# A transformer block: contexts turned and two head pairs' context keys projected before the self-attention, the last key block's values made in two pieces

## The chip, the cores and the metric

The kernel runs on one core of one Trainium2 chip. The time is that of one execution on the device, in microseconds. TensorE (PE, with its weight loads PEld) multiplies and turns, VectorE (DVE), ScalarE (ACT) and GpSimd (POOL) do the rest, and the DMA queues of SyncE (SP) and ScalarE load and store.

## The reference

Everything is float32. x is (2, 1024, 256): two sequences of 1024 tokens. The context is (2, 154, 192). With 16 heads of 64:

```
h = layernorm(x, ln1);  x = attention(h, h,       sa_wq, sa_wk, sa_wv, sa_wo, sa_bo) + x
h = layernorm(x, ln2);  x = attention(h, context, ca_wq, ca_wk, ca_wv, ca_wo, ca_bo) + x
h = layernorm(x, ln3);  a, gate = split(h @ ff_w1 + ff_b1)
out = (a * gelu(gate)) @ ff_w2 + ff_b2 + x
```

Attention is softmax(q k^T / 8) v per head. The keys and values of the second attention are projections of the context alone (ca_wk, ca_wv: 192 x 1024), so they depend on nothing that the first attention computes.

## The kernel before

The heads go in pairs, eight pairs for each of two sequences: 16 units. A unit of self-attention has eight slots, each of which makes the scores of two groups of queries against all 1024 keys (`scores`, L526, two buffers), takes the maximum on VectorE (L712), the exponents on ScalarE (L537), exchanges maxima and sums between partitions by four small DMAs on SyncE (L547), scales on GpSimd (L650) and turns on VectorE (L675). Beside this TensorE does, in an order written out by hand, the work that other slots left: projections of the next unit's queries, keys and values (L369, L405, L431), the product with the values (L578), the output projection (L500). `run_work` takes, in a slot, from a list `work` first and then one entry of a list `side`. An engine executes its instructions in the order in which the program issues them.

Before the first slot stands a beginning of its own. x comes in four loads of two tiles each on the queues of SyncE and ScalarE (`load_x`), then the gain and shift of the first normalisation, element by element into the columns `cols` (L110), then the weights. DMAs take turns over eight semaphores, so that each one is issued only when the eighth before it has landed. TensorE passes the time with 27 transposes of the identity (L1293). `norm_pieces` gives the statistics (L242, L243), the deviation (L248, L252), the normalising (L273 on GpSimd, L276 on ScalarE) and the turning (L286) with the copy to hT (L297 on VectorE, L301 on ScalarE) for pairs of tiles, and the beginning issues these in between the first unit's queries and keys, for a quarter of the tokens at a time (`part`, in the banks `first` and `first_k`).

The context enters as follows. `turn_context` turns both sequences' contexts into ctxT (L203), `context_keys` projects one pair's keys into kT (L792), and `turn_rows` (L194) turns the rows of the other gains and biases into columns. These stand in `side` for the first four slots. Of a context's 154 rows the last block of 32 is kept apart: `context_ends` (L813) projects it for both sequences and both halves of the heads, 128 columns at a time, into `ends`; its weights come by `load_ends` (L803), both in the self-attention's units 5 to 8 (L1355 to L1360), a piece in the seventh slot of each.

`xt[1, 1]` (the second half of the second sequence's x) is loaded only from the second unit on, and `held_v[:, 1]` and `held_v[:, 3]` (values) are first written in the first two units.

Of the kernel before, what the change touches and what calls it, by code (L numbers as in the profile page):

```python
# [13 lines left out]
P = 128  # L14
# [4 lines left out]
def tile_transformer_block(ctx: ExitStack, tc: tile.TileContext, a: dict, out: bass.AP):  # L19
# [19 lines left out]
    KP = T // 2  # L39
    KB = 32  # L40
    NB = -(-T // KB)
    EC = P
    VC = 2 * P
    HB = 512
    QG = 2 * KB
# [34 lines left out]
        for b in range(B) for g in range(NG)  # L80
    }

    def load_x(queue, b, t):

        queue.dma_start(
            out=xt[b, t // GT][:, t % GT:t % GT + 2, :],
            in_=x[b, t * P:(t + 2) * P, :].rearrange("(t p) d -> p t d", p=P),
        )

# [12 lines left out]
            n_cols = r + k  # L102
        r += k
    rows = pp_.tile([n_rows - n_cols, P], F32, tag="P", name="rows")
    for t in range(0, NT // 2, 2):
        load_x(nc.sync, 0, t)
        load_x(nc.scalar, 0, NT // 2 + t)
    for n in names[:2]:
        for r0 in range(0, P, HR):
            (nc.scalar if n == names[0] else nc.sync).dma_start(  # L110
                out=cols[r0:r0 + HR, row_of[n]:row_of[n] + NH],
                in_=w[n].rearrange("(r p) -> p r", p=HR),
            )
    bias = {}

    def load_bias(n):
# [56 lines left out]
    cn = []  # L173
    for b in range(B):
        cn.append(pp_.tile([KP, 2, DC], F32, tag="P", name=f"cn{b}"))
        nc.sync.dma_start(out=cn[b], in_=cond[b].rearrange("(t p) d -> p t d", p=KP))
    load_bias("sa_bo")

    power = const.tile([P, 2], F32, tag="power", name="power")
    nc.gpsimd.memset(power, -0.5)  # L180
    ident = const.tile([P, P], F32, tag="ident", name="ident")
    make_identity(nc, ident)

# [27 lines left out]


    ends = const.tile([P, DA // 2], F32, tag="ends", name="ends")
    held_v = const.tile([P, 4, NT, P], F32, tag="held_v", name="held_v")

    hT, vs, qk, oT = {}, {}, {}, {}

# [577 lines left out]
            )  # L795
        return lambda: nc.scalar.copy(kT[:, pr, :], pk[:, :B * TP])

    def load_ends(f, n):

        t = wpool.tile([CC, 2, 2, n], F32, tag="ck", name=f"ca_wv_{f}")  # L800
        own = w["ca_wv"].rearrange("(c p) (h f) -> p c h f", p=CC, h=2)
        for c in range(2):
            nc.sync.dma_start(out=t[:, c], in_=own[:, c, :, f:f + n])  # L803
        wsl["ends", f] = t

    def context_ends(f, n, bank):

        pe = bank(f"pe_{f}")
        for c in range(2):
            for b in range(B):  # L810
                for half in range(2):
                    r0 = (2 * b + half) * KB
                    nc.tensor.matmul(  # L813
                        pe[r0:r0 + KB, :n], lhsT=ctxT[:, c, (b + 1) * TP - KB:(b + 1) * TP],
                        rhs=wsl["ends", f][:, c, half, :], start=(c == 0), stop=(c == 1),
                        tile_position=(0, r0),
                    )
        return lambda: nc.scalar.copy(ends[:, f:f + n], pe[:, :n])
# [447 lines left out]
    with tc.manual_schedule():  # L1266
# [3 lines left out]
        def emit(*pieces):  # L1270
            for piece in pieces:
                run(piece)
            flush(stores)
# [15 lines left out]
                      i * P, 2 * P, shared=True)  # L1289


        for _ in range(27):
            nc.tensor.transpose(own[0][:, 1, :P], ident, ident)  # L1293
# [30 lines left out]
        work.extend(unit_value_piece(*units[0], i, 2) for i in (0, 2))  # L1324

        for p in range(SA):
# [26 lines left out]
            else:  # L1353
                run_work(2 if p < SA - SH else 1, h % 2 or h == 0, sum_tile)
            if hg == LAG:  # L1355
                f = (ui - NPAIR // 2 - 1) * EC
                if n == LAG and 0 <= f < DA // 2:
                    load_ends(f, min(EC, DA // 2 - f))
                elif n == SH + LAG and 0 <= f < DA // 2:
                    run(lambda: context_ends(f, min(EC, DA // 2 - f), sum_tile))  # L1360
                if n == SH + LAG and ui in (0, 1, NU - 1):

                    pr = {0: 2, 1: 4, NU - 1: 6}[ui]
                    run(lambda: context_keys(pr, sum_tile))
                    kept.append(context_keys(pr + 1, mm_tile))
# [175 lines left out]
```

## Time and profile before

| | us |
|---|---|
| median of 3 runs | 1068.17 (1067.32 to 1068.81) |
| profiled execution | 1067.09 |
| its span | 1065.1 |
| TensorE busy | 1055.6 (99%) |
| VectorE busy | 882.5 (83%) |
| GpSimd busy | 778.4 (73%) |
| ScalarE busy | 647.3 (61%) |
| DMA | 57 GB/s in the mean |

Times in the profile count from the span's start; the profiled execution is the span and what lies around it. The chain of waits follows the work that ended last back from the last instruction, at each step to what released it; a change shows in the end only where it touches this chain. In the timeline a row is a group of like instructions in a row: its start, its length, engine, line, operation, tiles, count, and in brackets how long the engine had been idle and what released it. The ends of matmuls are modelled, so a busy TensorE can hide a short wait. The granted clock of TensorE reads 1.00 in every stretch.

### The profile page before, as it was taken

To read this page: it belongs to the slowest core of one execution; us is meant where nothing else is said; L and a number is where in the kernel's file an instruction comes from. 1 tells how busy PE (TensorE), PEld (TensorE's weight loads), DVE (VectorE), ACT (ScalarE), POOL (GpSimd) and SP (SyncE) were. 2 spreads that over 40 slices of the span, in tenths; PEclk is the share of its full clock that TensorE was granted. 3 is DMA by queue.
4 is the path that set the end of the run, shared out by engine and by line. 5 is a ranking of instruction groups with operands and counts; after the bars stand their busy time and mean duration, and the time that the engine had idled before them with its cause. 6 is when DMAs were issued, how large, how long until landed. Compare 5 with 4: busy or idle time off the path is not lost.

```text
span 1065.1 us, 48669 instructions
## 1 busy us (share of the span) xinstructions
PE 1055.6 (99%) x20228; PEld 707.7 (66%) x20228; DVE 882.5 (83%) x1321; ACT 647.3 (61%) x2096; POOL 778.4 (73%) x1652
## 2 busy tenths in 40 slices
PE   8999999999999999999999999999999999999998
PEld 6556656656555555667655655566866668788998
DVE  5789999998989989999999899979877877654555
ACT  5766767677666666666776676666666554343231
POOL 2677777778777777777777777777767875499984
PEclk9999999999999999999999999999999999999999
DMA  3131122121021121111102101126776545000000
GB/s 102 36 75 54 29 68 54 25 63 41 22 58 28 34 51 34 39 34 34 45 14 54 44 14 38 33 57 161 175 172 165 123 98 125 5 11 11 21 10 30
DMA packets 86046, 60.95 MB, mean 57 GB/s; under 512 B 32123, under 2 KB 74563, under 8 KB 85827
## 3 DMA queue, kind: packets, MB, share of 16 engines
q1 hardware_dynamic: 84450, 57.07, 22.1%
q8 instruction: 159, 2.61, 1.0%
q10 hardware_dynamic: 1376, 0.79, 0.3%
q14 instruction: 61, 0.49, 0.2%
HBM read 27.91 MB, written 2.10 MB: 28 GB/s over the span
## 4 chain that ended last, share of the span: by engine, by line
PE 90%; DVE 3%; POOL 2%; DMA 2%; SPq 1%; issue 1%; ACT 1%; DVEq 0%; POOLq 0%; ACTq 0%
PE po L578 19%; PE s L526 19%; PE py_ca L500 5%; PE py_sa L500 5%; PE pk_sa L369 5%; PE pq_sa L369 5%; PE pq_ca L369 4%; PE pv_sa L405 4%; PE poc L953 4%; PE pb L1074 4%; PE pq L1219 4%; PE sc L873 3%; PE pa L1074 2%; PE pc L1074 2%; PE pf L1249 1%; PE ph_ln L286 1%
## 5 line engine op out<-in xcount | busy, mean ns | idle before, releaser
L650 POOL TENSOR_SCALAR p<-p,rd,ee 128x512 f32<-128x512 f32 x512 | 392.6, 772 | 88.6 <-DVE rd L640 86.6
L537 ACT ACTIVATE p<-s,st 128x512 f32<-128x512 f32 x512 | 345.3, 687 | 174.1 <-DVE st L712 170.6
L712 DVE TENSOR_REDUCE st<-s 128x2 f32<-128x1024 f32 x256 | 308.7, 1207 | 57.7 <-issue 17.5
L675 DVE STREAM_TRANSPOSE pT<-p 128x1024 f32<-128x1024 f32 x256 | 302.5, 1219 | 1.6 <-POOL p L650 1.4
L526 PE MATMUL s<-k_sa,q_sa 64*32 64x512 f32 x4096 | 255.8, 591 | 0.8 <-DVE k_sa L390 0.6
L578 PE MATMUL po<-pT,held_v 64*32 64x256 f32 x8192 | 238.9, 376 | 0.0
L578 PEld LDWEIGHTS po<-pT,held_v 64*32 64x32 f32 x8192 | 178.2, 106 | 69.8 <-issue 26.5
L526 PEld LDWEIGHTS s<-k_sa,q_sa 64*32 64x32 f32 x4096 | 87.4, 106 | 93.1 <-issue 46.8
L890 ACT ACTIVATE p<-sc,neg 128x154 f32<-128x154 f32 x256 | 96.4, 406 | 73.5 <-DVE rden L898 70.6
L901 POOL TENSOR_SCALAR p<-p,rden 128x154 f32<-128x154 f32 x256 | 97.3, 401 | 47.3 <-DVE rden L898 47.0
L537 ACT ACTIVATION_READ_ACCUMULATOR p<-s,st 128x1 f32 x512 | 103.7, 203 | 0.0
L555 POOL TENSOR_TENSOR dd<-st 128x8 f32<-128x8 f32 x128 | 25.8, 202 | 69.0 <-DMA st<-st 65.1
L500 PE MATMUL py_ca<-ca_wo,o_ca 128*128 128x256 f32 x256 | 60.2, 383 | 0.0
L500 PE MATMUL py_sa<-sa_wo,o_sa 128*128 128x256 f32 x256 | 59.5, 386 | 0.0
L500 PEld LDWEIGHTS py_sa<-sa_wo,o_sa 128*128 128x128 f32 x256 | 47.3, 190 | 18.0 <-issue 5.9
L369 PE MATMUL pq_ca<-hT_ln,ca_wq 64*64 64x512 f32 (+1 forms) x576 | 58.5, 589 | 0.3 <-DMA ca_wq<-in_L_xattn_ca_wq_dram 0.3
L879 DVE TENSOR_REDUCE neg<-sc 128x6 f32<-128x924 f32 (+1 forms) x48 | 47.8, 995 | 12.1 <-PE sc L873 12.1
L369 PE MATMUL pq_sa<-hT_ln,sa_wq 64*32 64x512 f32 (+1 forms) x976 | 57.3, 586 | 0.0
L890 ACT ACTIVATION_READ_ACCUMULATOR p<-sc,neg 128x1 f32 x256 | 56.7, 221 | 0.0
L369 PE MATMUL pk_sa<-hT_ln,sa_wk 64*32 64x512 f32 x960 | 56.5, 590 | 0.1
L917 DVE STREAM_TRANSPOSE pT_ca<-p 128x480 f32<-128x480 f32 (+1 forms) x96 | 52.9, 586 | 0.9 <-POOL p L901 0.8
L500 PEld LDWEIGHTS py_ca<-ca_wo,o_ca 128*128 128x128 f32 x256 | 47.4, 190 | 8.2 <-issue 1.9
(158 smaller groups left out, 1479.5 us busy)
## 6 DMA issues: line engine op xcount, KB each, us to landing
wf<-pT_ca SPq DMA_DIRECT2D x128, 128.0 KB, 2.4
st<-st SPq DMA_DIRECT2D x512, 1.0 KB, 1.8
held_v<-held_v SPq DMA_DIRECT2D x32, 256.0 KB, 3.8
sa_wq<-in_L_xattn_sa_wq_dram SPq DMA_DIRECT2D x32, 128.0 KB, 2.9
sa_wk<-in_L_xattn_sa_wk_dram SPq DMA_DIRECT2D x32, 128.0 KB, 3.3
sa_wv<-in_L_xattn_sa_wv_dram SPq DMA_DIRECT2D x16, 256.0 KB, 4.3
ca_wq<-in_L_xattn_ca_wq_dram SPq DMA_DIRECT2D x32, 128.0 KB, 3.7
wf<-in_L_xattn_ff_w_dram SPq DMA_DIRECT2D x12, 256.0 KB, 3.1
```

What stands on the lines that cost most here:

```text
L369: nc.tensor.matmul(pq[r][f:f + m, at:at + n], lhsT=wt[own, c, f:f + m], rhs=h[own, c, t0:t0 + n], start=(c == 0), stop=(c == NH - 1), tile ...
L500: nc.tensor.matmul(py[:, e * D:(e + 1) * D], lhsT=o[:, i, (t + e) * P:(t + e + 1) * P], rhs=wo[kind][:, g * HP + i, :], start=(i == 0), st ...
L526: nc.tensor.matmul(sc[a4 * KB:(a4 + 1) * KB, j, :], lhsT=q[r, c:c + KB], rhs=k[r, h * HB:(h + 1) * HB], start=True, stop=True, tile_positi ...
L537: nc.scalar.activation(pr[:, j, :], sc[:, j, :], AF.Exp, bias=st[:, 0, 0, i, j:j + 1], accum_out=st[:, 0, 1, i, j:j + 1],)
L578: nc.tensor.matmul(po[a2][d:d + KB, :QH // 2], lhsT=v[e][r, t, d:d + KB], rhs=pT[r, d // DH * NK + n, :], start=(t == 0 and e == 0), stop= ...
L650: nc.gpsimd.tensor_scalar(pr[:, j, :], pr[:, j, :], own["rd"][:, c:c + 1], own["ee"][:, 0, c:c + 1], op0=ALU.mult, op1=ALU.mult,)
L675: nc.vector.transpose(halves[h][:, :, c:c + KB], slots[p]["p"][i].rearrange("p j (n k) -> p (j n) k", k=KB))
L712: nc.vector.tensor_reduce(st[:, 0, 0, i, :], sc[i], AX.X, ALU.max, negate=True)
L890: nc.scalar.activation(pr_[:, j, i, :T], sc[:, j, i * T:(i + 1) * T], AF.Exp, bias=neg[:, j, i:i + 1], accum_out=den[:, j, i:i + 1],)
L901: nc.gpsimd.tensor_scalar(pr_[:, j, i, :T], pr_[:, j, i, :T], rden[:, j, i:i + 1], 1.0, op0=ALU.mult, op1=ALU.mult,)
L917: nc.vector.transpose(pTc["ring"][:, ui % 3, :, j, t0 * KB:(t0 + nt) * KB].rearrange("p n (i q) -> p i n q", q=KB), pr_[:, j, :nt, :].rear ...
L1074: nc.tensor.matmul(into[:, :BT], lhsT=lhs, rhs=wh[pair][i], start=first, stop=True, skip_group_check=True)
```

## The change

- x's first four tiles come in loads of one tile each, the others in two loads of two, in an order that is held; both contexts come behind the first tile on each queue, and the first two pairs' ca_wk (`first_keys`) on ScalarE's queue. A small activation (`ready`) follows on ScalarE.
- The gain and shift of the first normalisation come as eight rows into `held_v[:, 3]`, are turned by one transpose and copied to `cols`.
- TensorE's beginning: 12 warming transposes, both contexts turned, 4 more, the first pair's context keys, the turned gains, then the transposes of x as before, but with the second turning behind the first part of the queries and the third behind the second part. The second pair's context keys come behind the last keys of the first unit.
- ca_wv is loaded whole, its two halves of rows into `xt[1, 1]` and `held_v[:, 1]`. `context_ends` takes 256 columns (EC doubled) and stands in `side` twice, behind `turn_rows`: second and third slot. `load_ends` and its eight loads are gone.

```diff
-    EC = P
+    EC = 2 * P
...
+    end_weights = [
+        t[:CC].rearrange("p t d -> p (t d)").rearrange("p (h f) -> p h f", h=2)
+        for t in (xt[B - 1, NG - 1], held_v[:, 1])
+    ]
...
+    rows1 = held_v[:n_cols, 3, 0, :]
...
+    with tc.manual_schedule():
+        load_x(nc.sync, 0, 0, 1)
+        load_x(nc.scalar, 0, NT // 2, 1)
+        for own, src, queue in zip(cn, cond, (nc.sync, nc.scalar)):
+            queue.dma_start(out=own, in_=src.rearrange("(t p) d -> p t d", p=KP))
+        load_x(nc.sync, 0, 1, 1)
+        load_x(nc.scalar, 0, NT // 2 + 1, 1)
+        load_x(nc.sync, 0, 2, 2)
+        first_keys = wpool.tile([CC, 2, 2 * P], F32, tag="ck", name="ca_wk_0")
+        nc.scalar.dma_start(
+            out=first_keys, in_=w["ca_wk"][:, :2 * P].rearrange("(c p) f -> p c f", p=CC))
+        ready = small.tile([P, 2], F32, tag="off", name="ready")
+        nc.scalar.activation(ready, power, AF.Identity)
+        for n in names[:2]:
+            nc.sync.dma_start(
+                out=rows1[row_of[n]:row_of[n] + NH, :].rearrange("r (i f) -> r i f", f=HR),
+                in_=w[n].rearrange("(r p) -> r p", p=HR).unsqueeze(1).broadcast_to([NH, 2, HR]),
             )
+        load_x(nc.sync, 0, NT // 2 + 2, 2)
...
+    for c in range(2):
+        nc.sync.dma_start(
+            out=end_weights[c],
+            in_=w["ca_wv"][c * CC:(c + 1) * CC, :].rearrange("p (h f) -> p h f", h=2))
...
-                        rhs=wsl["ends", f][:, c, half, :], start=(c == 0), stop=(c == 1),
+                        rhs=end_weights[c][:, half, f:f + n], start=(c == 0), stop=(c == 1),
...
-        for _ in range(27):
-            nc.tensor.transpose(own[0][:, 1, :P], ident, ident)
-        emit(stats[0], stats[1], deviation[0])
-        emit(stats[2], stats[3], normalize[0], deviation[1], stats[4], normalize[1])
-        copies = [turn[0](), turn[1]()]
+        def keys(pr, bank):
+            wsl["ca", pr, "k"] = first_keys[:, :, pr * P:(pr + 1) * P]
+            return context_keys(pr, bank)
+
+        warm(12)
+        spare["bank"] = mm_tile
+        for turned in [turn_context(b) for b in range(B)]:
+            turned()
+        spare["bank"] = sum_tile
+        warm(4)
+        emit(stats[0], stats[1], deviation[0], stats[2], normalize[0])
+        done = keys(0, mm_tile)
+        nc.tensor.transpose(own[1][:, 1, :n_cols], rows1, ident[:n_cols, :n_cols])
+        nc.scalar.copy(cols[:, :n_cols], own[1][:, 1, :n_cols])
+        copies = [turn[0]()]
+        emit(stats[3], deviation[1], stats[4])
         copies[0]()
+        emit(normalize[1])
+        done()
         part("q", 0)
+        copies.append(turn[1]())
         part("k", 0)
         emit(stats[5], deviation[2])
         copies[1]()
         emit(stats[6], normalize[2], stats[7], deviation[3])
+        part("q", 1)
         copies = turn[2]()
-        part("q", 1)
+        part("k", 1)
         emit(normalize[3])
         copies()
-        part("k", 1)
         copies = turn[3]()
         banks["k2"] = two_banks("first_k")
         part("k", 2)
...
         part("k", 3)
+        done = keys(1, sum_tile)
         take("k", 2)
-        load_keys(0, 2)
+        done()
...
-        side.append((True, (), lambda: together(*(lambda b=b: turn_context(b) for b in range(B)))))
-        side.extend((True, (), lambda pr=pr: context_keys(pr, sum_tile)) for pr in range(2))
         side.append((True, (), turn_rows))
+        side.extend((True, (), lambda f=f: context_ends(f, min(EC, DA // 2 - f), sum_tile))
+                    for f in range(0, DA // 2, EC))
...
-                f = (ui - NPAIR // 2 - 1) * EC
-                if n == LAG and 0 <= f < DA // 2:
-                    load_ends(f, min(EC, DA // 2 - f))
-                elif n == SH + LAG and 0 <= f < DA // 2:
-                    run(lambda: context_ends(f, min(EC, DA // 2 - f), sum_tile))
```

More of the change, by code (lines that the diff above doesn't have):

```diff
@@ L104, in tile_transformer_block @@
     rows = pp_.tile([n_rows - n_cols, P], F32, tag="P", name="rows")
[L105 to L112, printed above, removed]
+    cn = [pp_.tile([KP, 2, DC], F32, tag="P", name=f"cn{b}") for b in range(B)]
+    rows1 = held_v[:n_cols, 3, 0, :]
+    power = const.tile([P, 2], F32, tag="power", name="power")
+    nc.gpsimd.memset(power, -0.5)
+    with tc.manual_schedule():
[15 more added lines that the diff above has]
+                in_=w[n].rearrange("(r p) -> r p", p=HR).unsqueeze(1).broadcast_to([NH, 2, HR]),
             )
+        load_x(nc.sync, 0, NT // 2 + 2, 2)
     bias = {}
@@ L796, in context_keys @@
         return lambda: nc.scalar.copy(kT[:, pr, :], pk[:, :B * TP])
[L798 to L804, printed above, removed]
     def context_ends(f, n, bank):
@@ L1289, in take, with warm @@
                       i * P, 2 * P, shared=True)
-        for _ in range(27):
-            nc.tensor.transpose(own[0][:, 1, :P], ident, ident)
-        emit(stats[0], stats[1], deviation[0])
-        emit(stats[2], stats[3], normalize[0], deviation[1], stats[4], normalize[1])
-        copies = [turn[0](), turn[1]()]
+        def warm(n):
+            for _ in range(n):
+                nc.tensor.transpose(own[0][:, 1, :P], ident, ident)
+        def keys(pr, bank):
[13 more added lines that the diff above has]
+        emit(stats[3], deviation[1], stats[4])
         copies[0]()
+        emit(normalize[1])
+        done()
         part("q", 0)
+        copies.append(turn[1]())
         part("k", 0)
```

14 lines of the change are left out of this document (4 added, 10 removed).

## The prediction

> **What bounds the kernel now.** I read the page first, for the shares of the engines.
>
> ```profile
> span 1065.1 us, 48669 instructions
> PE 1055.6 (99%) x20228; PEld 707.7 (66%) x20228; DVE 882.5 (83%) x1321; ACT 647.3 (61%) x2096; POOL 778.4 (73%) x1652
> L578 PE MATMUL po<-pT,held_v 64*32 64x256 f32 x8192 | 238.9, 376 | 0.0
> ```
>
> TensorE is busy for 1055.6 of 1065.1 us, so an instruction taken from it shows in the end, if it lay in a stage where TensorE itself ends last. Whether it does is read from the chain of waits, in order of time; here are its pieces at the beginning (start, length, what).
>
> ```profile
> 0.72 3.48 DMA x<-in_x_dram
> ...
> 6.82 0.56 POOL xn_ln L273
> ...
> 8.29 0.73 DVE hT_ln L297 x2
> ...
> 11.10 0.57 POOL xn_ln L273
> ...
> 12.40 1.99 PE first L369 x32
> 14.39 0.58 PE ph_ln L286 x4
> 14.97 2.04 PE first_k L369 x32
> ...
> 17.03 0.44 DVE k_sa L390
> ...
> 17.61 1.95 PE s L526 x32
> 19.56 1.93 PE pq_sa L369 x16
> 21.48 0.67 PE pc L203 x8
> ...
> 24.04 1.99 PE pv_sa L431 x32
> 26.03 1.27 PE pk L792 x4
> ...
> 31.17 1.27 PE pk L792 x4
> ...
> 37.75 0.17 PE p_rows L194
> ...
> 48.95 0.64 PE s L526 x9
> ```
>
> Up to 12.4 us the end is set by a latency chain (load of x, statistics, normalising, turning), beside a TensorE with time to spare. From 12.40 to 49.59 it is TensorE alone: the context's turning (0.67), two projections of context keys (1.27 each) and the turning of the rows (0.17) all lie on the path. In the middle, where the four pieces of `ends` are made (units 5 to 8), the same view gives:
>
> ```profile
> by line: PE s L526 33.4%; PE po L578 32.6%; PE py_sa L500 8.4%; PE pk_sa L369 8.2%; PE pv_sa L405 8.0%; PE pq_sa L369 7.9%; PE pe L813 1.3%; PE ph_ln L286 0.5%
> 389.11 3.65 PE py_sa L500 x16
> 392.76 0.57 PE pe L813 x16
> 393.34 1.88 PE s L526 x32
> 395.22 3.45 PE po L578 x128
> ...
> 431.37 3.65 PE py_sa L500 x16
> ...
> 473.20 3.65 PE py_sa L500 x16
> ```
>
> The first row is the share by line from 270 to 400 us: nothing but TensorE. A piece costs 0.57. The unit with one runs from 389.11 to 431.37, 42.26; the next, without, to 473.20, 41.83. So leaving one out is worth 0.43 to 0.57.
>
> **The change, part by part.** All terms are against the profiled execution, 1067.09 us with 2.0 around its span; that is 1.08 under the median of the runs shown, 1068.17, to which I add the sum.
>
> *Units 5 to 8.* Four pieces go: 4 x 0.57 = -2.28 (by the other bound 4 x 0.43 = -1.72). I take 0.57, the piece's own row on the chain: scores, with nothing between, follow it. Four ScalarE copies and eight SyncE loads go with them; neither stood on the chain there, so nothing is counted.
>
> *Second and third slot.* Each loses a projection (1.27) and gets a piece of 256 columns. Its price is not in the trace. A value matmul of the same 256 columns takes 238.9 us / 8192 = 0.029 with eight tiles at a time; a piece is 16 matmuls with four at a time, 16 x 0.058 = 0.93, and 0.06 to 0.13 of edges (0.57 for 128 columns is twice 0.22 and 0.13). I take 0.99, between 0.57 (as if width were free) and 1.14 (twice 0.57). So 2 x (0.99 - 1.27) = -0.56. Both halves of ca_wv (0.79 MB, 2.1 us at 385 GB/s) are now loaded at the beginning, where the contexts stood on SyncE's queue:
>
> ```profile
> 13.36 0.37 SPq L118 DMA_DIRECT2D sa_bo<-in_L_xattn_sa_bo_dram  x1
> 22.92 3.23 SPq L547 DMA_DIRECT2D st<-st  x4
> ```
>
> The issue after them was at 13.36, the next work of that queue, the first exchange of maxima, at 22.92, and the first piece reads them at about 26: ten us to arrive, nothing queued behind them that is waited for: hidden. If they came after 26, TensorE would stop in the second slot.
>
> *First and fourth slot.* In the first the context's turning (0.67) makes room for that of the rows (0.17), which leaves the fourth: -0.50 and -0.17. But the first is not all mine to keep:
>
> ```profile
> 22.12 0.69 ACT L537 ACTIVATE p<-s,st 128x512 f32<-128x512 f32 x1
> 22.95 0.18 PEld L526 LDWEIGHTS s<-k_sa,q_sa 64*32 64x32 f32 x16 [0.69 <-ACT p L537]
> ```
>
> The second half of the next scores waits for the bank that the exponents of the first slot release at 22.8; it starts at 22.95, with 0.1 to 0.2 to spare at most. Arriving 0.50 earlier it waits 0.32 of it: -0.18 remains (bounds 0 and -0.50).
>
> *The beginning.* TensorE's order is now: 12 warming transposes, context turned, 4 more, first keys, the gains' rows, and only then the first transposes of x.
>
> ```profile
> 1.91 5.67 PE L1293 MATMUL first<-ident 128*128 128x128 f32 x27 [1.91 <-POOL ident masks.py:199]
> 7.49 0.63 PE L286 MATMUL ph_ln<-ident,xn_ln 128*128 128x128 f32 x4
> 9.01 0.63 PE L286 MATMUL ph_ln<-ident,xn_ln 128*128 128x128 f32 x4 [0.90 <-POOL xn_ln L273]
> L1293 PEld LDWEIGHTS first<-ident x27: 141/230/230, 1.9 to 7.2; 128*128 128x128 f32 x27
> ```
>
> The warming transposes come every 0.21 us with 230 ns of weight load, and the last few with 141: TensorE gets its full pace only near 6.9. So: 12 x 0.21 from 1.91 ends at 4.43; the context's turning, 0.67 x 230/141 = 1.09, at 5.52; four more at 6.36; keys 1.27, of which 0.54 us pass at the slow pace (0.33 of the work), at 7.84; the rows 0.17, at 8.0. The first transposes of x start at 8.0, not 7.49: +0.5, whatever the loads gain. The loads:
>
> ```profile
> 4.22 0.43 DVE L242 BATCH_NORM_STATS2 st_ln<-x 128x6 f32<-128x256 f32 x1 [4.22 <-DMA x<-in_x_dram]
> ...
> 6.75 0.60 ACT L276 ACTIVATE xn_ln<-x,off_ln,rstd_ln 128x256 f32<-128x256 f32 x1 [1.20 <-DVE off_ln L258]
> ...
> 9.57 1.16 PE L369 MATMUL first<-hT_ln,sa_wq 64*128 64x128 f32 x16
> 2.25:2.50 0.25, 0.25 (x3) 0.25 (x2) 0.00 (x0) 0.00 (x0) 0.00 (x0) 1.00 1.02 197
> 3.50:3.75 0.25, 0.25 (x3) 0.25 (x2) 0.00 (x0) 0.00 (x0) 0.00 (x0) 1.00 1.11 385
> SPq L134 <- DMA x<-in_x_dram: 1.8, 2, 1.4
> ```
>
> 0.52 MB of x had landed at 4.22. With 0.26 MB ahead of the first statistics these start 0.26 / 0.385 = 0.7 earlier, at 3.5; the contexts (0.23 MB more) land near 4.1, as the 12 transposes end; ca_wk, last of 1.19 MB, at 4.22 + 0.67 / 0.385 = 6.0, before 6.36. (The two rows by time are stretches: in the last column GB/s.) The weights wait on SyncE for the eighth transfer before them (the last row: it waited for x), now behind three more issues of x and gains, about 1 us; sa_wq is read only after hT, near 8.9 (9.57 before), and its issue at some 5 us leaves it 4. The statistics and the normalising took from 4.22 to 7.38; from 3.5 on the same 3.16 end at 6.7, before a TensorE busy until 8.0: what the loads gain is not used, and if x came 1.3 us later still, nothing would be lost. The table load on ScalarE, now beside these loads, and the two memsets ahead of them are hidden by the same wait for x.
>
> Then hT starts near 8.5 (8.29 before), after two of the four transposes and the copy of the turned gains on ScalarE, which takes the place of four loads element by element. The second pair's offset now stands behind these two copies (0.73) on VectorE, its normalising (0.6) after that, so its transposes start 1.6 after hT, not 0.72 (9.01): normalising of the third pair, 11.10 before, is at 12.0. That costs little: q's second part (half of the 1.99 at 12.40) fills TensorE meanwhile, and only k's second part stands between the third and fourth turning; first_k ends at 17.0 as before. Behind it the second projection of keys (1.27) covers the wait for the copy (17.03 to 17.61): scores start at 18.26. +0.65 (bounds: 0, if hT comes 0.65 earlier; +1.2, if none of the slip is made good).
>
> Sum: -2.28 - 0.56 - 0.18 - 0.17 + 0.65 = -2.54. 1068.17 - 2.54 = 1065.6 us, 0.24% under. About 0.2%, 2.1 us, is what a measurement of this kernel can tell from no change.
>
> **The clock.** The Trainium skill (TensorE: Matmul & The Clock Gate, Part 4) says that transposes do not count as activity that releases the full clock. The row above disagrees: the pace rises within 27 transposes, with no matmul of data before. By the rule the old kernel would have stayed slow until its projections at 9.6, and the change, with keys at 6.4, would gain about 1 us more; the sum goes by the row. Part 1 of the same page says that the clock rises after a busy window of about 3.4 us, free-running; no row here shows the window itself, and the rival below is what it would do.
>
> **The rivals.** *Late clock.* Gaps (waits for contexts, for ca_wk) keep TensorE from its full pace for as long again as it took, 6.9 - 1.91 = 5 us. Matmuls then take 230/141 as long: 5 x (1 - 141/230) = 1.9 where TensorE is the path, perhaps 1.5. 1067.1, no change. For it: three waits where there was unbroken work. Against: each is under 0.3 us by the sum above.
>
> *The first slots give nothing.* ScalarE has as much to do as before in slots 1 to 3 (a copy of `ends` for one of the keys), and if its exponents set the pace, -0.56 and -0.35 fall away; with 0.43 for a piece: +0.65 - 1.72 = -1.07, 1067.1. For it: the scores' wait above. Against: the chain is TensorE's from 17.61 to 49.59.
>
> *More than forecast.* Transposes of x at 7.5, since the pace rises earlier, and scores that don't wait: 0 - 0.50 - 0.56 - 0.17 - 2.28 = -3.5, 1064.7.
>
> *Slower.* The keys stand before x's transposes in TensorE's order, so a late ca_wk holds up everything. At the 197 GB/s of the early row, 1.19 MB from 1.9 takes until 7.9 and the start goes 1.6 back: 1067.2. From a landing at 6.36 + 2.54 = 8.9 on the change loses; at 11.2, 4.84 later than reckoned, it gives 1070.4. For it: nothing else lies between; the contexts and ca_wk are in the way of x as well. Against: 385 GB/s from 3.0 on.
>
> **How the numbers follow.** Forecast 0.45, its own range 1065.0 to 1066.3, four fifths of it faster by over 0.2%; more than forecast 0.17, faster; first slots give nothing 0.18 and late clock 0.12, both no change; slower 0.08. Faster 0.36 + 0.17 = 0.53, no change 0.09 + 0.30 = 0.39, slower 0.08. The range goes from 1064.0 (below the better case by the spread of the forecast) to 1068.2 (a late clock at 1.9 with pieces at 0.43).
>
> **What would show it.** The first scores at 18.3, not 17.6; x's first transposes near 8.0 with the keys just before them; the second half of the second slot's scores waiting for ScalarE; pieces of `ends` 0.99 each on TensorE; units 5 to 8 of 41.8 instead of 42.3. Wrong, if weight loads of 230 ns go on past 8 us, if the keys wait for ca_wk, or if a piece of 256 columns takes over 1.2.

## The result and the profile after

The changed kernel took 1070.51 us in the median of 22 executions (1066.40 to 1073.19), the kernel before, run beside it, 1068.37 us (1067.00 to 1070.64, 22 executions). The ratio is 1.0018, with a 95% interval of 1.0011 to 1.0026: by the ratio, as for all differences to the kernel before from here on, 1.9 us slower (the medians themselves lie 2.1 apart). That is just under the 0.2% that the prediction names as the least to be told from no change, though the interval leaves no doubt of its sign; 2.5 us less were forecast (1065.6, in a range to 1068.2). Two later measurements of the same kernel gave 1.0025 (1.0010 to 1.0039) and 1.0011 (1.0000 to 1.0022).

The profile must be read with this in mind: the profiled execution took 1066.40 us, which is the shortest of the 22. It shows what the change costs at best. The page:

```profile
span 1064.6 us, 48582 instructions
PE 1054.2 (99%) x20186; PEld 696.4 (65%) x20186; DVE 882.6 (83%) x1321; ACT 646.5 (61%) x2096; POOL 775.1 (73%) x1652
```

TensorE has 42 matmuls and 1.4 us less, its weight loads take 11.3 us less, GpSimd 3.3; the rest differs by under 1. The chain of waits of the first 60 us (start, length, what):

```profile
2.22 5.32 DMA ca_wk<-in_L_xattn_ca_wk_dram
7.54 0.14 issue
7.67 1.31 PE pk L809 x4
...
16.63 1.99 PE first_k L386 x32
18.62 1.27 PE pk L809 x4
19.89 1.10 PE s L543 x16
...
22.86 2.21 ACT p L554 x7
25.07 0.04 issue
25.11 1.09 PE s L543 x16
...
28.19 1.00 PE pe L822 x16
...
33.06 1.00 PE pe L822 x16
...
35.93 3.94 PE pq_sa L386 x64
39.87 1.72 PE s L543 x32
```

The chain no longer begins with x but with ca_wk: the load of the first keys' weights was issued at 2.22 and landed at 7.54. The first scores start at 19.89; before it was 17.61. By the chain the four first slots then take 39.87 - 19.89 = 19.98, against 37.92 - 17.61 = 20.31 (37.75 and 0.17 from the row of `p_rows`). But a row of the chain begins only where the row before it ends, and matmuls of the two can run side by side. The timeline gives the starts themselves, before:

```profile
37.68 0.24 PE L194 MATMUL p_rows<-ident,rows 28*128 28x28 f32 x1
37.85 1.98 PE L526 MATMUL s<-k_sa,q_sa 64*32 64x512 f32 x32
```

and after:

```profile
35.84 4.03 PE L386 MATMUL pq_sa<-hT_ln,sa_wq 64*32 64x512 f32 x64
39.30 2.29 PE L543 MATMUL s<-k_sa,q_sa 64*32 64x512 f32 x32
```

The scores of the fifth slot start at 39.30, beside the last queries; before, the turning of the rows stood between the two. By the timeline the first scores start at 19.82, and the four slots take 39.30 - 19.82 = 19.48, against 37.85 - 17.61 = 20.24: 0.76 less.

TensorE ahead of them, from the timeline:

```profile
5.63 0.76 PE L1303 MATMUL first<-ident 128*128 128x128 f32 x4
7.67 1.31 PE L809 MATMUL pk<-ctxT,ca_wk 96*128 96x320 f32 x4 [1.28 <-DMA ca_wk<-in_L_xattn_ca_wk_dram]
...
9.07 0.66 PE L303 MATMUL ph_ln<-ident,xn_ln 128*128 128x128 f32 x4
10.09 1.26 PE L386 MATMUL first<-hT_ln,sa_wq 64*128 64x128 f32 x16 [0.36 <-DVE hT_ln L314]
```

It stood idle for 1.28 us ahead of the first keys, and x's first transposes, behind them in its order, started at 9.07 instead of 7.49. The busy time by stretches says why ca_wk was late (last column GB/s):

```profile
4.00:5.00 1.00, 1.00 (x8) 0.75 (x7) 0.83 (x4) 0.19 (x1) 0.02 (x1) 1.00 0.95 284
5.00:6.00 1.00, 1.00 (x9) 1.00 (x8) 0.34 (x1) 0.54 (x2) 0.69 (x1) 1.00 0.94 277
6.00:7.00 1.00, 0.39 (x4) 0.16 (x2) 0.90 (x6) 0.88 (x2) 0.55 (x1) 1.00 0.98 268
```

The DMA engines are nearly as busy (0.94 to 0.98) as in the row of 385 GB/s in the prediction (1.11), but move 268 to 284 GB/s. Last, the middle, by the chain of waits, where the four pieces of `ends` went:

```profile
263.82 3.65 PE py_sa L517 x16
...
431.83 3.65 PE py_sa L517 x16
```

The corresponding first row of the kernel before:

```profile
261.25 3.65 PE py_sa L500 x16
```

Units 5 to 8 take 431.83 - 263.82 = 168.01, against 431.37 - 261.25 = 170.12.

### The profile page after: what moved, and what is told of

It reads as the page before. It is cut to its first block, busy times and chain, and to the rows that moved or that the text cites. A ratio compares the mean times of both kernels' runs of the same rounds, so it can differ in the third digit from the quotient of the medians.

```text
span 1064.6 us, 48582 instructions
## 1 busy us (share of the span) xinstructions
PE 1054.2 (99%) x20186; PEld 696.4 (65%) x20186; DVE 882.6 (83%) x1321; ACT 646.5 (61%) x2096; POOL 775.1 (73%) x1652
## 4 chain that ended last, share of the span: by engine, by line
PE 93%; DVE 2%; DMA 1%; POOL 1%; ACT 1%; issue 1%; SPq 0%; ACTq 0%; DVEq 0%; POOLq 0%
PE po L595 20%; PE s L543 20%; PE py_sa L517 5%; PE py_ca L517 5%; PE pq_sa L386 5%; PE pk_sa L386 5%; PE pq_ca L386 5%; PE pv_sa L422 4%; PE pb L1083 4%; PE poc L962 4%; PE pq L1228 4%; PE sc L882 3%; PE pa L1083 2%; PE pc L1083 2%; PE pf L1258 1%; PE ph_ln L303 1%
## 5 line engine op out<-in xcount | busy, mean ns | idle before, releaser
L595 PEld LDWEIGHTS po<-pT,held_v 64*32 64x32 f32 x8192 | 175.6, 106 | 73.4 <-issue 27.9
L422 PE MATMUL pv_sa<-sa_wv,hT_ln 64*32 64x256 f32 x1792 | 52.8, 376 | 0.0
```

What stands on the lines that cost most here:

```text
L422: nc.tensor.matmul(pv[r][f:f + KB, e * VC:(e + 1) * VC], lhsT=h[half, c, t0:t0 + KB], rhs=wt[half, c, :], start=(c == 0), stop=(c == NH - ...
L595: nc.tensor.matmul(po[a2][d:d + KB, :QH // 2], lhsT=v[e][r, t, d:d + KB], rhs=pT[r, d // DH * NK + n, :], start=(t == 0 and e == 0), stop= ...
```

## The experiments

The four first runs were made for four theories: A, the wait for ca_wk; B, TensorE's pace, late or lost; C, the loss arises in the exchange of the softmax sums behind the first slots; D, the pieces of `ends`. The later ones use other letters: A there is the idle time that costs TensorE its pace, L the late landing by itself, C as before. In the table, the times of the kernel before are those of the same chip; the last two columns are from the profiled execution of each: the start of the first scores in the timeline, and how long the first 16 matmuls of the queries took (17.61 and 1.16 before, 19.82 and 1.26 in the profile on record).

| | run | median, us | before, us | ratio (95%) | scores | queries |
|---|---|---|---|---|---|---|
| 1 | changed kernel again | 1073.26 | 1070.21 | 1.0025 (1.0010 to 1.0039) | 22.51 | 2.15 |
| 2 | pieces alone, old beginning | 1069.86 | 1070.21 | 1.0001 (0.9991 to 1.0011) | 17.74 | 1.16 |
| 3 | new beginning alone | 1072.54 | 1070.21 | 1.0015 (1.0004 to 1.0026) | 19.33 | 1.26 |
| 4 | first keys later | 1072.44 | 1070.21 | 1.0014 (1.0004 to 1.0024) | 21.68 | 2.25 |
| 5 | gap filled | 1069.93 | 1069.84 | 1.0000 (0.9988 to 1.0012) | 19.62 | 1.26 |
| 6 | gap in the old kernel | 1073.02 | 1069.84 | 1.0033 (1.0021 to 1.0045) | 20.37 | 2.08 |
| 7 | gains earlier, x first | 1069.47 | 1069.84 | 1.0000 (0.9989 to 1.0011) | 20.15 | 1.71 |
| 8 | slots 2 and 3 padded | 1073.48 | 1069.84 | 1.0035 (1.0021 to 1.0048) | 22.01 | 2.15 |
| 9 | x's second pair of tiles first | 1068.46 | 1069.80 | 0.9989 (0.9979 to 0.9999) | 22.17 | 2.08 |
| 10 | gap filled, again | 1069.63 | 1069.80 | 0.9996 (0.9986 to 1.0005) | 20.02 | 1.26 |
| 11 | changed kernel, third time | 1070.87 | 1069.80 | 1.0011 (1.0000 to 1.0022) | 22.07 | 2.15 |
| 12 | as 9, less idle time | 1066.97 | 1069.21 | 0.9981 (0.9971 to 0.9992) | 21.41 | 1.69 |

### 1. The changed kernel again

> The changed kernel once more, for a second profile and its times: the profile on record shows a start 2.3 us late and yet an end 0.5 earlier, while the median of its runs is 2.1 above the kernel before. Theory A (the first keys wait for ca_wk, and all of x's transposes stand behind them): the median stays near 1070.5, the first keys start at 7.5 or later in this profile too, the weight loads of the transposes are at 140 ns by 7 us, the first scores start near 20. Theory B (TensorE's full pace rises late in most executions, because waits break its early work): weight loads of 200 ns and more are seen past 8 us, and the first scores start at 21 or later. Theory C (the loss lies behind the first slots, in the exchange of maxima): the start is as on record and the unit periods up to unit 5 are longer than 42.4 us.

Measured: 1073.26 against 1070.21, and this time a profile of an execution with 1074.35. TensorE in it, from the timeline:

```profile
8.13 1.72 PE L809 MATMUL pk<-ctxT,ca_wk 96*128 96x320 f32 x4 [2.00 <-DMA ca_wk<-in_L_xattn_ca_wk_dram]
...
9.98 1.11 PE L303 MATMUL ph_ln<-ident,xn_ln 128*128 128x128 f32 x4
11.25 2.15 PE L386 MATMUL first<-hT_ln,sa_wq 64*128 64x128 f32 x16 [0.15 <-DVE hT_ln L314]
```

and two of its stretches (the number before the last two is the granted clock):

```profile
8.00:9.00 1.00, 0.87 (x3) 0.68 (x4) 0.48 (x2) 0.00 (x0) 0.00 (x0) 0.95 0.98 188
9.00:10.00 1.00, 1.00 (x4) 0.20 (x2) 0.00 (x0) 0.00 (x0) 0.00 (x0) 0.50 0.63 153
...
15.00:16.00 1.00, 1.00 (x14) 1.00 (x14) 0.90 (x6) 0.87 (x2) 0.51 (x1) 0.63 0.93 274
```

Four transposes of x take 1.11, not 0.66, and 16 matmuls of the queries 2.15, not 1.26. The granted clock is 0.50 from about 8.9 (0.95 in 8 to 9: the last tenth of it) to about 15.7 (0.63 in 15 to 16). The first scores come 2.7 us later than in the profile on record, and 4.9 later than before. The idle time ahead of the keys was 2.00. So the pace, the speed at which TensorE gets through like matmuls, is lost in some executions, and the profile on record is of one that kept it.

### 2 and 3. The two halves of the change

Run 2 keeps the old beginning and makes the two pieces in the fifth and sixth slot; run 3 has the new beginning and the old four pieces.

```diff
 # run 2, from the kernel before
...
+        side.extend((True, (), lambda f=f: context_ends(f, min(EC, DA // 2 - f), sum_tile))
+                    for f in range(0, DA // 2, EC))
...
 # run 3, from the changed kernel
...
-        side.extend((True, (), lambda f=f: context_ends(f, min(EC, DA // 2 - f), sum_tile))
-                    for f in range(0, DA // 2, EC))
+                f = (ui - NPAIR // 2 - 1) * EC
+                if n == LAG and 0 <= f < DA // 2:
+                    load_ends(f, min(EC, DA // 2 - f))
+                elif n == SH + LAG and 0 <= f < DA // 2:
+                    run(lambda: context_ends(f, min(EC, DA // 2 - f), sum_tile))
```

> The old beginning with the new ends: ca_wv whole at the beginning, two pieces of 256 columns behind the old side work, so in the fifth and sixth slot; units 5 to 8 without pieces. By the rows: 4 x 0.57 away, 2 x 1.00 added: -0.3, so 0.9997 of the kernel before. If the ends were what loses (theory D: 0.79 MB of early loads, or pieces in early slots), 1.001 to 1.003 with a first-slots stretch that is longer by more than 2.0.

> The new beginning with the old ends in units 5 to 8. Theories A and B: the whole loss is here; by additivity with the ends (-0.3) the ratio is 1.002 to 1.003. Theory D: 0.999 to 1.000.

The pieces alone change nothing that can be measured (1.0001), as four pieces of 0.57 against two of 1.00 should. The beginning alone loses 1.6 us (0.4 to 2.8; a ratio of 1.002 to 1.003 was expected, 1.0015 came), though it takes two projections of 1.27 out of the slots and adds nothing to them. So the loss comes with the beginning. In the profiled execution of run 3 ca_wk landed at 7.05, TensorE waited 0.57 for it, and the pace held.

### 4. The first keys behind the first unit's keys

```diff
-        done = keys(0, mm_tile)
         nc.tensor.transpose(own[1][:, 1, :n_cols], rows1, ident[:n_cols, :n_cols])
...
         part("k", 1)
+        done = keys(0, mm_tile)
         emit(normalize[3])
         copies()
+        done()
```

> The changed kernel with the first pair's context keys moved from in front of x's first transposes to behind the second part of the first unit's keys, so that nothing of x stands behind ca_wk. Theory A: x's first transposes start near 7 instead of 9.1, the first scores at 18.3 to 18.8 instead of 19.9, and the median is 1.1 to 1.6 under the changed kernel's. Theory B: the pace rises as late or later (less early work), the first scores near 20 still, no gain. Theory C: the start gains 1.1 to 1.6 and the end does not.

The wait for ca_wk is gone from TensorE's order, and yet no clear gain is seen: 1.0014, against 1.0025 for the changed kernel on the same chip and 1.0018 on record, with intervals that overlap. The first scores came at 21.68, not at 18.3 to 18.8. From the timeline:

```profile
8.08 0.20 PE L1316 MATMUL first<-ident,held_v 8*128 8x8 f32 x1 [1.47 <-DMA held_v<-in_L_xattn_ln_b_dram]
8.21 0.66 PE L303 MATMUL ph_ln<-ident,xn_ln 128*128 128x128 f32 x4
9.23 2.25 PE L386 MATMUL first<-hT_ln,sa_wq 64*128 64x128 f32 x16 [0.36 <-DVE hT_ln L314]
```

What was next in line was late too: the gains' rows landed at 7.94, TensorE was idle for 1.47, and a little later the pace halved, here for 3.4 us. This is what a wait replaced by the next one looks like.

### 5 and 10. The gap filled

```diff
-        warm(4)
+        warm(12)
```

> The changed kernel, with 12 instead of 4 transposes of the identity between the contexts' turning and the first keys. At the granted clock of 1.00 the eight added ones take about 1.3 us (four of x's transposes took 0.66), so that TensorE is busy to about 7.7 and no longer idle for 1.28 to 2.00 us ahead of the first keys. Theory A (the idle time lets the granted clock fall to 0.50 in part of the executions, and this makes the changed kernel slow): every execution has a mean clock of 1.000 (13 of 22 and 7 of 12 had less), the first scores start near 19.9, and the time falls by the mean cost of the falls, 1 to 2 us, to a ratio of about 1.0005 to 1.0012. Theory L (the late landing of the first keys' weights costs its 2.3 us in every execution, the clock adds nothing that lasts): clock 1.000 too, but the ratio stays at 1.0018 to 1.0025. Theory C (the loss arises in the exchange behind the first slots): the ratio stays as well, and waits for q_sa, held_v or the exchange stand between 36 and 107 us.

> The kernel of the run with 12 transposes in the gap once more, on the same chip as the changed kernel. Theory A: 1.5 to 2.5 us under the changed kernel, and x's first transposes at full pace (0.66 for four). Theories L and C: within 0.5 us of it.

Eight more transposes of the identity, which nobody reads. The timeline of run 5:

```profile
5.19 1.48 PE L1303 MATMUL first<-ident 128*128 128x128 f32 x12
7.47 1.32 PE L809 MATMUL pk<-ctxT,ca_wk 96*128 96x320 f32 x4 [0.80 <-DMA ca_wk<-in_L_xattn_ca_wk_dram]
...
8.87 0.66 PE L303 MATMUL ph_ln<-ident,xn_ln 128*128 128x128 f32 x4
```

ca_wk is as late as ever, x's transposes start at 8.87, the first scores at 19.62; and the kernel is level with the kernel before (1.0000 and 0.9996; for run 5 theory A had 1.0005 to 1.0012). In both profiles the pace held, and the mean granted clock was 1.000 in all 24 executions. By itself that clock rules out a fall and not a late rise (run 11 below). The changed kernel, with the gap, had 0.998 or less in 13 of 22, 7 of 12 and 3 of 11. Beside each other on one chip, run 10 is 1.24 us under run 11; 1.5 to 2.5 were expected, so this lies below the lower end, and the intervals of the two overlap. The theory L (the landing alone) would have left 1.0018.

### 6. The gap in the old kernel

```diff
-        for _ in range(27):
+        for _ in range(12):
```

> The kernel before, with 12 instead of 27 transposes of the identity at the beginning, so that TensorE is idle from about 5.2 to x's first transposes near 7.5, and again from 8.1 to 9.0 as before. Nothing else is touched. Theory A: the granted clock falls below 1.00 in part or all of the executions (it was 1.000 in all 35 of the kernel before), the first scores come 1.5 to 3.5 us later where it falls, and the time is 1 to 3 us above the kernel before, ratio 1.001 to 1.003. Theories L and C: the transposes of the identity write nothing that is used, and the ratio stays within 1.000 +- 0.001.

The old kernel with 15 warming transposes less is 3.5 us slower (2.2 to 4.8), a little over the 1 to 3 us expected. Timeline:

```profile
7.57 0.63 PE L286 MATMUL ph_ln<-ident,xn_ln 128*128 128x128 f32 x4 [2.83 <-POOL xn_ln L273]
9.08 1.09 PE L286 MATMUL ph_ln<-ident,xn_ln 128*128 128x128 f32 x4 [0.89 <-POOL xn_ln L273]
10.10 2.08 PE L369 MATMUL first<-hT_ln,sa_wq 64*128 64x128 f32 x16
```

The first transposes of x stand where they always stood and are fast; the second take 1.09, the queries 2.08, and the first scores come at 20.37, 2.8 late, with no load moved and nothing else changed on any engine. So idle time at this place costs this much by itself. The profile is of the one execution of the six with a mean clock under 1.000; the other five were as slow (1072.43 to 1074.29 us in all), and whether their pace rose late isn't shown.

### 7. The gains' rows earlier, x ahead of the keys

```diff
             queue.dma_start(out=own, in_=src.rearrange("(t p) d -> p t d", p=KP))
+        for n in names[:2]:
+            nc.sync.dma_start(
+                out=rows1[row_of[n]:row_of[n] + NH, :].rearrange("r (i f) -> r i f", f=HR),
+                in_=w[n].rearrange("(r p) -> r p", p=HR).unsqueeze(1).broadcast_to([NH, 2, HR]),
+            )
         load_x(nc.sync, 0, 1, 1)
...
-        warm(4)
+        warm(8)
...
-        done = keys(0, mm_tile)
         nc.tensor.transpose(own[1][:, 1, :n_cols], rows1, ident[:n_cols, :n_cols])
...
         copies = [turn[0]()]
+        done = keys(0, mm_tile)
```

> The changed kernel, with the two DMAs of the first LayerNorm's gains and biases issued ahead of x's second tile on SyncE's queue, the first head pair's keys placed behind x's first transposes instead of ahead of them, and 8 instead of 4 transposes of the identity. x's first transposes should start near 7.2 (xn_ln was there at 6.98), the keys near 7.9, the first scores at 18.4 to 19.0 against 19.89. Theory L (the start is what was lost): the time falls by 0.9 to 1.5 us against the changed kernel, to a ratio of 1.0005 to 1.0012; with A, where the idle time goes too, to 0.999 to 1.000. Theory C: the first scores come earlier and the end of the first unit (py_sa, 136.46) does not, the ratio stays at 1.0018 to 1.0025.

The first scores came at 20.15, not 18.4 to 19.0. The two small loads cost x its place: the timeline has

```profile
3.39 1.34 SPq L85 DMA_DIRECT2D x<-in_x_dram  x3
```

where these loads were issued from 1.63 on before; the statistics that read them waited 1.95 us and x's first transposes started at 7.99. At 1.0000 it was still under the changed kernel, with eight warming transposes in the gap for four. That is the upper end of theory A's range (0.999 to 1.000), but not by the start that was expected for it. The 1.71 us of the first queries hold a wait and no slow pace: x's transposes took 0.63 and 0.66, and the granted clock stayed at 1.00.

### 8. Slots 2 and 3 padded

```diff
         pe = bank(f"pe_{f}")
+        for _ in range(8):
+            nc.tensor.transpose(pe[:, n:n + P], ident, ident)
```

> The changed kernel with eight transposes of the identity ahead of each of the two pieces of the last key block's values, so that self-attention's second and third slots hold 1.3 us more of TensorE's work each, as much as the keys that the change took out of them (1.27 each). Where TensorE sets the pace of the first unit: both slots 4.86 -> 6.1 to 6.2, and 2.5 us more in all, ratio 1.0042 to 1.005. Theory C (the first unit is paced by the exchange of the softmax sums, SyncE's queue and DMA, as much as by TensorE, so that what is taken out of the first slots comes back as waits for q_sa, held_v and the exchange by 107 us): both slots are longer, but the waits behind them go, py_sa starts at 136 to 138 all the same, and the ratio stays under 1.003.

The second padded slot takes 38.22 - 32.33 = 5.89 in the timeline, instead of 4.87:

```profile
32.33 1.95 PE L543 MATMUL s<-k_sa,q_sa 64*32 64x512 f32 x32
...
36.20 1.09 PE L819 MATMUL pe<-ident 128*128 128x128 f32 x8
...
38.22 1.95 PE L543 MATMUL s<-k_sa,q_sa 64*32 64x512 f32 x32
```

Two slots by some 1.03 are 2.06 us, 0.0019; on top of 1.0011 to 1.0025 this gives 1.0030 to 1.0044, and 1.0035 was measured, where 1.0042 to 1.005 was expected of a first unit paced by TensorE and under 1.003 of theory C. The interval (1.0021 to 1.0048) excludes neither. `py_sa` started at 142.17, not at 136 to 138 as C had it, but after a start of the scores that was itself 2.2 late; in run 1, without the padding, it started at 142.63. So the run speaks against C as it was put, and doesn't settle how much of what the change took from the slots is kept.

### 11. The changed kernel for the third time

> The changed kernel once more, beside the two above. Ratio 1.0018 to 1.0025 as twice before; whether TensorE's pace is halved in the profiled execution is open (it was in one of two), but in part of the executions the mean granted clock is under 1.000 as before (20 of 34).

Its profile shows the second way to lose the pace. Timeline, and one stretch:

```profile
5.55 1.06 PE L1303 MATMUL first<-ident 128*128 128x128 f32 x4
7.33 2.47 PE L809 MATMUL pk<-ctxT,ca_wk 96*128 96x320 f32 x4 [0.71 <-DMA ca_wk<-in_L_xattn_ca_wk_dram]
9.93 1.11 PE L303 MATMUL ph_ln<-ident,xn_ln 128*128 128x128 f32 x4
11.20 2.15 PE L386 MATMUL first<-hT_ln,sa_wq 64*128 64x128 f32 x16 [0.16 <-DVE hT_ln L314]
```

```profile
8.00:9.00 1.00, 1.00 (x3) 0.67 (x2) 0.00 (x0) 0.00 (x0) 0.00 (x0) 1.00 0.86 210
```

ca_wk was there by 7.3 and the wait short (0.71), yet the keys took 2.47 for 1.31, and half pace lasted until about 14.5. Here the pace had not yet risen when the gap came, and did not rise for some 7 us more; and the granted clock reads 1.00 throughout, as it did in the kernel before while its first transposes went at half pace. The profile of run 8 is of this kind as well. So the mean granted clock tells only of a pace that was gained and lost; one that comes late must be read from the lengths of the matmuls. With this it fits that the 13 executions on record with a mean clock under 1 are no slower (median 1070.29) than the 9 with 1.000 (1070.88), though only one of the 22 has a profile to read the pace from.

Runs 10 and 11 were taken on one chip, and their profiles show how far a late start carries: 2.05 us apart at the first scores (20.02 and 22.07), 1.57 at the first `py_sa` (136.56 and 138.13), 1.87 at the one after unit 8 (433.48 and 435.35), 1.57 at the last (719.39 and 720.96). Only in what follows does run 10 lose the rest of it (spans of 1068.5 and 1068.7); one pair of profiles doesn't tell why.

### 9 and 12. A beginning that waits for less

From the changed kernel, x's second pair of tiles is loaded ahead of the contexts and the gains' rows ahead of x's third tile; the contexts are turned behind 16 transposes, x's first transposes stand ahead of the first keys, and the context's copies behind the normalising on ScalarE. Run 12 has 18 transposes for 16, and one in place of the four.

```diff
...
-        warm(12)
+        warm(16)                      # run 12: 18
+        emit(stats[0], stats[1], deviation[0], stats[2], normalize[0])
         spare["bank"] = mm_tile
-        for turned in [turn_context(b) for b in range(B)]:
-            turned()
+        turned = [turn_context(b) for b in range(B)]
         spare["bank"] = sum_tile
         warm(4)                       # run 12: 1
-        emit(stats[0], stats[1], deviation[0], stats[2], normalize[0])
-        done = keys(0, mm_tile)
         nc.tensor.transpose(own[1][:, 1, :n_cols], rows1, ident[:n_cols, :n_cols])
-        nc.scalar.copy(cols[:, :n_cols], own[1][:, 1, :n_cols])
         copies = [turn[0]()]
+        for t in turned:
+            t()
+        nc.scalar.copy(cols[:, :n_cols], own[1][:, 1, :n_cols])
+        done = keys(0, mm_tile)
```

> The changed kernel with x's second pair of tiles loaded ahead of the contexts, the gains' rows ahead of x's third tile, 16 transposes of the identity, the contexts turned behind them, four more transposes, and x's first transposes ahead of the first head pair's keys. The first LayerNorm's rows should be ready near 6.7 and x's first transposes start at 6.7 to 7.4, the first scores at 18.2 to 18.9 against 19.62 to 19.89, and TensorE has no idle time over 0.8 us ahead of them, so that its pace does not fall (x's transposes 0.66 for four, the query's 16 matmuls 1.26). Theory A with the sum for the later stages (2.28 in units 5 to 8, 0.6 to 0.7 in the slots): 1.5 to 2.2 us under the kernel before, ratio 0.9980 to 0.9988. If the later stages' gain is lost again in the exchange (C): 1.000, as with the filling alone.

> The kernel with x's first pair of tiles ahead, with 18 transposes of the identity for 16, so that the 0.36 us of waiting for the contexts (5.59 to 5.95) is filled, and one in place of four behind the contexts. If any idle time ahead of the rise puts it off (in the profile of the kernel with 16 TensorE was still at half pace up to 14.4, with PEclk 1.00 throughout), the pace now rises between 5.4 and 8.7, four of x's transposes take 0.66 by then or by the second turning, x's first transposes start near 7.2, the first scores at 18.4 to 19.3 against 22.17, and the time falls by 0.5 to 1.5 us more, to a ratio of 0.9975 to 0.9985. If the rise comes late without idle time too, the first scores stay at 21 to 22 and the ratio at 0.999.

Run 9 is under the kernel before (0.9989, short of the 0.9988 expected), run 12 more clearly so (0.9981, 0.9971 to 0.9992): 2.0 us less, and 3.2 to 4.7 us less than the changed kernel by its three ratios, each to the kernel before on its own chip. Both profiles lost pace and missed the start that was expected, so that run 12's ratio lies in the expected range (0.9975 to 0.9985) is not shown to have the expected reason; its profile is of the slowest of its twelve executions (1069.96). Run 9, timeline:

```profile
5.95 1.26 PE L221 MATMUL pc<-ident,cn 77*96 77x77 f32 x8 [0.36 <-DMA cn<-in_ctx_dram]
...
8.20 1.11 PE L303 MATMUL ph_ln<-ident,xn_ln 128*128 128x128 f32 x4
```

A wait of 0.36 ahead of the rise, and half pace until about 14.4. Run 12, timeline:

```profile
7.05 0.65 PE L303 MATMUL ph_ln<-ident,xn_ln 128*128 128x128 f32 x4
7.54 1.24 PE L809 MATMUL pk<-ctxT,ca_wk 96*128 96x320 f32 x4
10.10 1.69 PE L386 MATMUL first<-hT_ln,sa_wq 64*128 64x128 f32 x16 [1.31 <-DMA sa_wq<-in_L_xattn_sa_wq_dram]
```

The pace was there at 7.05, x's transposes started 2 us earlier than in the changed kernel; but now the query's weights are what is late (1.31 us), and the pace fell again, from about 11.8 to 15.2. That the wait of 0.36 is what kept run 9 slow isn't shown: run 12 waited 0.49 at that place and had risen.

## Why the prediction was wrong

**The step that failed is "The beginning. ... +0.65".** Where the pace held, the first scores came 2.21 us later than before (19.82 for 17.61), and in three of five profiles 2 to 3 us more were lost. Three things in it.

*The pace.* The rival "late clock" was held off with "each [wait] is under 0.3 us by the sum above". The waits were 0.57 to 2.00 us in the profiles of this beginning, and in some of them TensorE was without its full pace for up to 7 us in the densest stretch of the beginning. Of the five profiles with this beginning and its gap (the one on record and runs 1, 3, 8 and 11) three were slow: first scores at 22.0 to 22.5, against 19.3 to 20.0 where the pace held (runs 5 and 10 among these), so 2.0 to 3.2 us. At 3 of 5, that is some 1.2 to 1.9 us in the mean, an estimate from five profiles, and filling the gap gained 1.2 (run 10 beside 11) to 1.9 and 2.7 us (1.0000 against 1.0018 and 1.0025, on other chips). The rival priced it at 1.9 us, counted 1.5 and gave it 0.12; its price was near and its chance was not. It had a pace that rises late, as in runs 8 and 11; the fall of a pace already risen, as in run 1, it did not have.

*The landing.* ca_wk was to land at 6.0, at 385 GB/s from 3.0 on; it landed at 7.05 to 8.0, with 268 to 284 GB/s between 4 and 7 in the profile on record (265 to 317 in run 1). I had taken the rate that x's loads reach for all loads. This is the mechanism of the rival "slower" (the keys hold up x behind them). The keys waited for ca_wk, which the prediction names as a sign of being wrong. It cost less than the 1.6 us worked out there for a landing at 7.9: x's first transposes came at 9.07 for 8.0, 1.07 late. The rest of the 1.56 over the forecast's 0.65 lies behind them. From x's first transposes to the first scores the forecast has 18.26 - 8.0 = 10.26; it was 10.75 in the profile on record, and 10.74 to 10.75 in runs 3, 5 and 10, with waits of 0.36 and 0.18 to 0.19 for the copies of the turned tiles. And first_k, which was to end "at 17.0 as before", ended at 18.62.

*The gains' rows*, which the forecast did not price as a load, landed at 7.94 in run 4. With the keys out of the way they were next to be late.

**What held.** The pieces: 1.00 each for 0.99 forecast. Units 5 to 8: -2.11 for -2.28. By the starts in the timeline slots 2 and 3 gave -0.27 each for -0.28, slot 4 -0.17 as forecast (5.48 to 5.31), and slot 1 -0.05 for -0.18, since the second half of the second scores waits for the exponents (0.23 in the timeline), as forecast: -0.76 in all for -0.91. So the rival "the first slots give nothing" did not come about there. Two slips of the working matter little: the loads up to ca_wk are 1.22 MB, not 1.19 (0.79 of x, 0.24 of contexts, 0.20 of ca_wk), and by its own terms the range ends at 1068.1.

**What the sum leaves out.** Start, slots and units 5 to 8 give +2.21 - 0.76 - 2.11 = -0.66 where the pace holds, and the kernel with the gap filled came to 0.0 and -0.4. Something more is lost in the first unit behind the four slots. From the fifth slot's scores to the first `py_sa` it is 95.78 before (37.85 to 133.63) and 97.09 after (39.30 to 136.39). Among the waits of TensorE there is, after:

```profile
99.77 3.01 PE L595 MATMUL po<-pT,held_v 64*32 64x256 f32 x100 [0.79 <-DMA held_v<-held_v]
```

The waits for `q_sa` and `held_v` between 70 and 122 us sum to 0.28 to 3.56 us in the ten profiles that have a new beginning and the new pieces (all but run 2, 3 and 6), 1.3 in the mean; to nothing in the kernel before and 0.32 in run 6, to 0.58 in run 3 and 1.60 in run 2. These are the waits that theory C names. So a part of C, about 1 us by this estimate from few profiles, may hold beside the pace. No run takes these waits away, and they aren't shown to come from the change. With them the 4.5 us between forecast (-2.54) and result (+1.9) add up: 1.2 to 1.9 of pace, 1.6 of start, 0.3 of slots and units, about 1 here.

**Unsettled.** Part of the scatter (4.6 us between executions of the kernel before on one chip, 9.1 of the changed one) comes from ScalarE standing behind the exchange near 73 to 78 us, in run 1:

```profile
76.95 0.21 ACT L578 ACTIVATE ee<-dd 128x8 f32<-128x8 f32 x1 [2.89 <-POOL dd L573]
```

The copy of the queries stands behind this row, and `pk_sa` on TensorE waited 1.83 for it. Run 2, with the old beginning, has the same wait (1.41); run 11, with the new one, does not have it. Whether the change makes it likelier can't be told from single profiles.

## What to carry to other kernels

Before an order that worked is changed at the start of a kernel, ask what each engine does while it waits: here 27 transposes of the identity, which look like idle time, were what kept TensorE at its pace, and a change that put waits for loads in their place lost more there (2.2 us at the first scores, and some 1.2 to 1.9 by the pace) than it saved in the slots and units that follow (0.8 and 2.1). Work that waits for a load belongs behind work that does not, and a gap that stays is better filled. And a profile is one draw: when it shows a loss of nothing and the median shows 2 us, profile again before looking for the loss in it.

## What the runs showed of the hardware

- A fall of the pace lasts for 3.4 us or twice that: worked out from the stretches with a granted clock between 0.5 and 1, it was half from 8.9 to 15.7 in run 1 (0.95 and 0.63) and from 8.6 to 15.4 in run 6 (0.78 and 0.81), and for 3.4 us in runs 4 and 12. The Trainium skill (TensorE: Matmul & The Clock Gate, Part 1) gives a free-running window of 3413 ns; these lengths agree with one and two of them.
- The Trainium skill (TensorE: Matmul & The Clock Gate, Part 1) has the pace fall after at least one idle window, and its section "Why this matters for your kernels" allows gaps up to about 3 us. Here idle times of 2.00 (run 1), 1.47 (run 4) and 1.31 us (run 12) were followed by a fall, and 2.83 and 0.89 close together in run 6; 1.28 in the profile on record and 1.36 in run 7 were not. The measurement decides: in part of the executions a fall follows gaps well under 3 us.
- The Trainium skill (TensorE: Matmul & The Clock Gate, Part 4) says that the full clock doesn't engage for transposes. In run 5 twelve of them took 1.48 us, 0.12 each, before any matmul that isn't a transpose; in the kernel before they took 0.21 each at first. Here, with float32 transposes of the identity and the contexts, the pace rises.
- The granted clock in the profile reads 1.00 while matmuls run at half pace, if the pace has not yet risen (run 11: keys 2.47 for 1.31).
